# Masked keys and copies of halves on GpSimd instead of VectorE, in the head of a four-layer program on one core

## The chip, the cores and the metric

The program runs on one core of one Trainium2 chip. A core has five engines that run side by side, each with its own queue of instructions, which it takes in order: TensorE (PE; its weight loads are listed apart as PEld), VectorE (DVE), ScalarE (ACT), GpSimd (POOL) and SyncE (SP), which here only issues DMAs. Engines wait for each other by semaphores. The metric is the device time of one execution in microseconds (us), as the median of several runs.

## What is computed

The input x has 4 sequences of 2048 tokens with 256 features, all float32. Four layers follow one another, each on the layer-normalised x, and each is added to x:

```python
x = x + delta_attention(layernorm(x))   # conv, silu, l2norm, delta rule over time, 16 heads of 16
x = x + experts(layernorm(x))           # router: 8 of 32 experts a token, and a shared one
x = x + state_space(layernorm(x))       # a scan over time with 16 states
x = x + quantised_linear(layernorm(x))  # blocks of 32 rounded to a 6-bit grid
```

The change lies in the first. There every head keeps a 16 x 16 state S, and goes through the tokens:

```python
v_new = (v_t - k_t @ S) * beta_t
S = S + outer(k_t, v_new)
o_t = q_t @ S
```

## The kernel before

**Tiling.** The tokens are cut into 16 blocks of 128 tokens of each of the 4 sequences (512 rows). A block has 8 chunks of 16 tokens. Inside a chunk the delta rule is solved as a small triangular system, so that only the step from chunk to chunk is a recurrence: 128 steps in all.

**Stages of a block i in the first layer.**

- `project(i)`: loads x, normalises it, transposes it (TensorE), multiplies it by the three weights, and makes the short convolution of each on VectorE (`cy`, lines 259 and 263: one scaling and three multiply-adds of 128 x 512). The results are kq (keys and queries, interleaved) and vh (values).
- `gram(i)`: the products of all keys and queries of a chunk with its keys, head by head. Line 348 makes `kqd`, a copy of the keys and queries of a chunk, four times over, each time with all but one head's features masked to zero (kq, repeated, times hmask: 128 x 512). Sixteen such tiles are made for a block, in four groups of four (`u0`); there are three buffers for them. Eight small matmuls (line 358) read each one into `pg`. ScalarE brings `pg` to `gk`, of which there is one buffer, and a DMA stores `gk` in `gscr`. `gram(0)` runs inside `project(0)` ahead of the values' convolution, the others at the end of `project(i)`.
- `substitute(i)`: loads the products back as `lq`, sets the tile `e` to zero (a memset on GpSimd, line 396; one buffer, so the memset waits until the earlier `e` has been stored), and solves the triangular systems in 16 pairs of multiply and add on VectorE (`step`, line 416, and `e`, line 422). The result goes to `escr`.
- `chain()`: the recurrence. `prepare` (lines 469 to 523) loads the chunk's solved system (`tm`), makes `twice`, a copy of the chunk's values and keys in which every column stands twice (line 475, two copies of 128 x 256, one buffer), transposes it on TensorE (`vk`, line 484), masks it on ScalarE (`vkm`, `kr`), and multiplies by `tm` (`c0`, line 505). Then `wr`, `wt` and `wq` (lines 512 to 521) prepare the product with the state. `finish` adds that product (line 529), copies it out as `ro` (line 535, ScalarE), makes the update (`sps`, line 542), and writes the new `state` (line 549, VectorE). `prepare` of a step is written ahead of `finish` of the step before.
- `normalise` and `output`: after every four chunks, and at the end of the block (`x`, line 596).

**Other work in the same time.** `route(i)` chooses the experts of a finished block (written beside block i + 1 of the recurrence) and scatters its rows by 32 indirect DMAs that GpSimd issues (line 799). Experts' tiles come in from block 4 on; each ends in two indirect DMAs of GpSimd that add to the sums (line 967). After the last block of the recurrence come the remaining experts and the last two layers, where GpSimd also makes three elementwise operations a block (lines 1094, 1095 and 1147).

**What sets the order.** The stages are generators. `weave` draws steps from them in turn: beside block i of the chain, `substitute(i + 1)` and `project(i + 2)` (beside block 0 also `project(1)`). The block of instructions so written is then put in its final order on every engine by a scheduler that works with estimated durations, so a change of engine at one place can move instructions of all engines anywhere behind it. In the final program each engine's order is fixed. In addition `beside` makes the scatters of line 799 wait for a `mark`, the last `ro` written ahead of them, to spread them over the block.

**Names for the change.** `GROUPS = (3, 5, 5, 3)` groups the 16 blocks for the experts; `GFIRST` holds the first block of each group, so `GFIRST[1]` is 3.

Of the kernel before, what the change touches and what calls it, by code (L numbers as in the profile page):

```python
# [42 lines left out]
GFIRST = [sum(GROUPS[:g]) for g in range(NGRP)]  # L43
# [131 lines left out]
def delta_layer(ctx, sh, nblk, layer, done, others):  # L175
# [11 lines left out]
    nc, tc, a = sh.nc, sh.tc, sh.a  # L187
# [43 lines left out]
    def project(i):  # L231
# [84 lines left out]
        if i == 0:  # L316
            yield from gram(i)
# [9 lines left out]
        if i > 0:  # L327
            yield from gram(i)

    def gram(i):  # L330

        kq = keys[i]
        gscr = sh.dram.tile([NB * C, NF, NU, NP, 2, 2 * C], F32, name="gscr")
        for u0 in range(0, NK, 2):
            f, u = u0 // NU, u0 % NU
            gk = work.tile([P, 2, NP, 2, 2 * C], F32, name="gk", bufs=1)
            pairs = gk.rearrange("p u (c h q) r t -> p h u c (q r t)", c=NC2, h=2)  # L340
            pg = [
                layer.mm.tile([P, 2, NC2, HH * 2 * C], F32, name=f"pg{h}", tag="mm")
                for h in range(2)
            ]
            for du, c in itertools.product(range(2), range(NC2)):

                kqd = work.tile([P, NB, HH, 2 * C], F32, name="kqd", bufs=3)
                nc.vector.tensor_tensor(  # L348
                    kqd,
                    kq[:, u0 + du, c].rearrange("p b t w -> p b (t w)")  # L350
                    .unsqueeze(2).broadcast_to([P, NB, HH, 2 * C]),
                    hmask.unsqueeze(1).unsqueeze(3).broadcast_to([P, NB, HH, 2 * C]),
                    op=ALU.mult,
                )
                for h in range(2):
                    rows = slice(h * 64, (h + 1) * 64)
                    for b in range(NB):
                        nc.tensor.matmul(  # L358
                            pg[h][b * 32 : (b + 1) * 32, du, c],
                            kq[rows, u0 + du, c, b].rearrange("p t w -> p (t w)"),  # L360
                            kqd[rows, b].rearrange("p h t -> p (h t)"),
                            start=True, stop=True,
                        )
            for h in range(2):
                nc.scalar.copy(pairs[:, h], pg[h])
            nc.sync.dma_start(gscr[:, f, u : u + 2], gk[0:P:2])
            yield
        grams[i] = gscr
# [66 lines left out]
    def load_t(i, g):  # L435

        t = tm[g % 2]
        f, u = g // 2, g % 2 * 2
        for b in range(NB):
            l = (b * 32 + u * NP) * 2 * C  # L440
            nc.sync.dma_start(
                t[b * 32 : (b + 1) * 32, :, :, b % 2].rearrange("j u p t -> j (u p) t"),
                outer[i][f, :, l : l + 2 * NP * 2 * C].rearrange("j (l t) -> j l t", t=2 * C),
            )

    def chain():

        parts = {0: prepare(0, 0)}
        for i in range(nblk):
            ot = work.tile([P, NC2, NB, T], F32, name="ot", bufs=1)  # L450
            for k in range(NK):
                n = i * NK + k + 1
                if n < nblk * NK:
                    parts[n] = prepare(*divmod(n, NK))
                    yield
                if k % NU == 0:
                    ro = work.tile([P, NU, DM], F32, name="ro", bufs=2)
                with tc.high_priority():
                    finish(i, k, *parts.pop(n - 1), ro[:, k % NU, :])
                yield  # L460
                if k % NU == NU - 1:
                    normalise(k // NU, ro, qsq[i], ot)
                    yield
            output(i, ot)
            yield

    def prepare(i, k):
        if k % 2 == 0:
            load_t(i, k // 2)
        kq, vh = keys[i], vals[i]  # L470
        tmk = tm[k // 2 % 2][:, k % 2]

        twice = work.tile([P, 2, NC2, NB * C, 2], F32, name="twice", bufs=1)
        for w, src in ((0, vh[:, k]), (1, kq[:, k, :, :, :, 0])):
            nc.vector.tensor_copy(
                twice[:, w],
                src.rearrange("p c b t -> p c (b t)")
                .unsqueeze(3)
                .broadcast_to([P, NC2, NB * C, 2]),
            )  # L480
        vk = layer.turn.tile([P, 2, NC2, P], F32, name="vk", tag="tr")
        for w in range(2):
            for c in range(NC2):
                nc.tensor.transpose(
                    vk[:, w, c, :], twice[:, w, c].rearrange("p n r -> p (n r)"), sh.ident
                )
        vkm = work.tile([P, 2, NP, 2, HD], F32, name="vkm")
        pairs = vk.rearrange("p w c (q r d) -> p (w c q) r d", r=2, d=HD)
        for r in range(2):
            nc.scalar.activation(  # L490
                vkm.rearrange("p w q r d -> p (w q) r d")[:, :, r, :], pairs[:, :, r, :],
                AF.Copy, scale=parity[:, r : r + 1],
            )
        kr = work.tile([P, 2, DM], F32, name="kr")
        for h in range(2):
            nc.scalar.activation(
                kr[:, h, :], vk[:, 1].rearrange("p c d -> p (c d)"),
                AF.Copy, scale=kmask[:, h : h + 1],
            )

        c0 = pc.tile([P, 2, DM], F32, name="c0")
        for p in range(NP):
            for h in range(2):
                rows = slice(h * 64, (h + 1) * 64)
                nc.tensor.matmul(  # L505
                    c0[rows, :, p * 32 : (p + 1) * 32],
                    tmk[rows, p].rearrange("p b t -> p (b t)"),
                    vkm[rows, :, p].rearrange("p w r d -> p w (r d)"),
                    start=(p == 0), stop=False, skip_group_check=True,
                )  # L510
        wr = work.tile([P, DM], F32, name="wr", bufs=1)
        nc.scalar.copy(wr, c0[:, 1])
        wt = layer.turn.tile([P, NC2, NB, C, 2], F32, name="wt", tag="tr")
        for c in range(NC2):
            nc.tensor.transpose(
                wt[:, c].rearrange("p b t w -> p (b t w)"), wr[:, c * P : (c + 1) * P],
                sh.ident,
            )
        wq = work.tile([P, NC2, NB, C, 2], F32, name="wq")
        nc.scalar.mul(wq[..., 0], wt[..., 0], -1.0)  # L520
        nc.vector.tensor_tensor(
            wq[..., 1], kq[:, k, :, :, :, 1], wt[..., 1], op=ALU.subtract
        )
        return c0, wq, kr
# [817 lines left out]
```

## Time and profile before

| | |
|---|---|
| median of 9 runs | 3637.48 us (3624.57 to 3655.48) |
| the profiled execution's own time | 3648.82 us |
| its span | 3647.0 us |
| granted TensorE clock in it, mean | 0.873 |
| VectorE: kqd (line 348) | 256 instructions, 168.7 us, mean 689 ns |
| VectorE: twice (line 475) | 256 instructions, medians 288 and 295 ns |
| GpSimd: all | 1235 instructions, 1721.5 us |
| GpSimd: indirect DMAs (lines 799 and 967) | 512 at 1030 ns, 640 at 1635 ns |
| GpSimd: elementwise with two inputs of 128 x 1024 (lines 1094, 1095, 1147) | 48, means 2710, 2743, 2454 ns |

The profile is of one execution. It gives each instruction's start and duration on its engine, what released it when it waited, and the line of the program that it comes from. The page sums this up: busy time by engine, busy tenths in 40 equal slices of the span (each 91 us), groups of instructions. Any stretch, line or tile can be asked for by itself. An instruction's recorded duration holds the time in which it stands still on its engine after it has begun. Starts are in us from the span's start.

### The profile page before, as it was taken

The numbers are of one execution on the slowest core, as the hardware profiler recorded it, in microseconds if no ns is written. First come the engines' busy times: TensorE is split into PE (matmuls) and PEld (weight loads), VectorE is DVE, ScalarE is ACT, GpSimd is POOL, SyncE is SP. The second block draws the span as 40 slices with busy tenths as digits, with TensorE's granted clock in tenths as the row PEclk, the third lists the DMA queues.
The fourth block names the chain that finished last, engine by engine and source line by source line (L and its number), as shares of the span: only waits on it lengthen the run. The fifth ranks groups of instructions, "written<-read, shape, count | busy, mean of one in ns | idle before, by whom it ended". The sixth has DMA issues, their size and how long they took to land. (4 is left out here: it accounts for less than half of the span.)

```text
span 3647.0 us, 72319 instructions
## 1 busy us (share of the span) xinstructions
PE 2943.3 (81%) x24564; PEld 2184.2 (60%) x24564; DVE 2017.2 (55%) x4958; ACT 1812.3 (50%) x3640; POOL 1721.5 (47%) x1235
## 2 busy tenths in 40 slices
PE   5778887888988888888888878677488999789844
PEld 2455555665666666566666656566267677567612
DVE  4785775564646455464655535234367644475476
ACT  4454444454545444464545545334265766467522
POOL 0004322545454452545445454545566788658711
PEclk7777887998989888999989889888699999999967
DMA  3334446777878787787777788758699999999910
GB/s 88 54 61 129 113 113 171 189 182 187 193 196 206 179 209 179 192 199 196 194 185 190 174 224 203 197 159 239 188 315 285 269 303 294 312 272 281 234 64 18
DMA packets 788811, 695.92 MB, mean 191 GB/s; under 512 B 482313, under 2 KB 672025, under 8 KB 785305
## 3 DMA queue, kind: packets, MB, share of 16 engines
q1 hardware_dynamic: 669432, 522.25, 50.6%
q0 software_dynamic: 116736, 167.85, 22.5%
q8 instruction: 195, 3.19, 0.4%
q14 instruction: 176, 1.43, 0.1%
q10 hardware_dynamic: 2272, 1.19, 0.1%
HBM read 472.41 MB, written 267.53 MB: 203 GB/s over the span
## 5 line engine op out<-in xcount | busy, mean ns | idle before, releaser
L967 POOL DMA_INDIRECT sum<-ye,wrow x640 | 1046.6, 1635 | 956.5 <-ACT ye L964 746.5
L946 PE MATMUL gu<-xe,we 128*128 128x128 f32 x5120 | 710.0, 294 | 49.8 <-ACT xe L936 22.7
L799 POOL DMA_INDIRECT rows<-xn,rows x512 | 527.3, 1030 | 464.6 <-issue 242.9
L946 PEld LDWEIGHTS gu<-xe,we 128*128 128x128 f32 x5120 | 664.1, 207 | 113.3 <-issue 56.2
L959 PE MATMUL py<-we,he 128*128 128x256 f32 x1280 | 367.5, 412 | 85.0 <-DVE he L952 72.4
L952 DVE TENSOR_TENSOR he<-he,gu 128x256 f32<-128x256 f32 x320 | 133.3, 417 | 495.6 <-ACT he L951 370.4
L964 ACT ACTIVATE ye<-py,wrow 128x256 f32<-128x256 f32 x640 | 267.9, 471 | 279.0 <-PE py L959 146.2
L959 PEld LDWEIGHTS py<-we,he 128*128 128x128 f32 x1280 | 233.1, 200 | 147.8 <-DVE he L952 84.0
L951 ACT ACTIVATE he<-gu 128x256 f32<-128x256 f32 x320 | 123.1, 385 | 354.6 <-PE gu L946 203.7
L934 PE MATMUL px<-ident,xg 128*128 128x128 f32 x1280 | 227.4, 289 | 76.2 <-DMA xg<-rows 63.3
L505 PE MATMUL c<-vkm,tm 64*64 64x64 f32 x4096 | 213.2, 240 | 81.0 <-issue 70.2
L348 DVE TENSOR_TENSOR kqd<-kq,hmask 128x512 f32<-128x512 f32 x256 | 168.7, 689 | 188.8 <-PE pg L358 85.8
L936 ACT COPY xe<-px 128x512 f32<-128x512 f32 x320 | 188.1, 588 | 145.8 <-PE px L934 117.6
L934 PEld LDWEIGHTS px<-ident,xg 128*128 128x128 f32 x1280 | 165.7, 148 | 150.5 <-issue 60.6
L505 PEld LDWEIGHTS c<-vkm,tm 64*64 64x64 f32 x4096 | 170.9, 149 | 129.5 <-issue 108.0
L358 PE MATMUL pg<-kqd,kq 64*32 64x128 f32 x4096 | 184.3, 323 | 64.2 <-issue 46.0
L263 DVE SCALAR_TENSOR_TENSOR cy<-pre,convw,cy 128x512 f32<-128x512 f32 x288 | 215.0, 751 | 3.5
L549 DVE TENSOR_TENSOR state<-sps,same 128x512 f32<-128x512 f32 x254 | 165.9, 684 | 83.9 <-remote 36.3
L247 PE MATMUL proj<-xt,wqkv 128*128 128x512 f32 x384 | 206.0, 663 | 1.0 <-issue 0.8
L542 PE MATMUL sps<-ro,kr 64*128 64x128 f32 x2032 | 166.7, 310 | 18.3 <-ACT ro L535 18.3
L358 PEld LDWEIGHTS pg<-kqd,kq 64*32 64x32 f32 x4096 | 94.9, 119 | 137.1 <-issue 94.1
L542 PEld LDWEIGHTS sps<-ro,kr 64*128 64x128 f32 x2032 | 140.5, 210 | 51.9 <-ACT ro L535 25.0
(206 smaller groups left out, 4990.8 us busy)
## 6 DMA issues: line engine op xcount, KB each, us to landing
we<-in_wexp SPq DMA_DIRECT2D x640, 384.0 KB
xg<-rows SPq DMA_DIRECT2D x640, 128.0 KB
sum<-in_blank SPq DMA_DIRECT2D x48, 512.0 KB
part<-sum SPq DMA_DIRECT2D x48, 512.0 KB
rows<-in_zeros SPq DMA_DIRECT2D x132, 160.0 KB
x<-in_x SPq DMA_DIRECT2D x32, 512.0 KB
gscr<-gk SPq DMA_DIRECT2D x64, 256.0 KB
lq<-gscr SPq DMA_DIRECT2D x64, 256.0 KB
```

Of the source, the lines that this page charges most:

```text
L247: nc.tensor.matmul(ps, wqkv[:, k, w, c * P : (c + 1) * P], xt[:, k, :], start=(k == 0), stop=(k == NC2 - 1),)
L263: nc.vector.scalar_tensor_tensor(y, pre[:, :, k : k + T], convw[:, w, c, k : k + 1], y, op0=ALU.mult, op1=ALU.add,)
L358: nc.tensor.matmul(pg[h][b * 32 : (b + 1) * 32, du, c], kq[rows, u0 + du, c, b].rearrange("p t w -> p (t w)"), kqd[rows, b].rearrange("p h ...
L505: nc.tensor.matmul(c0[rows, :, p * 32 : (p + 1) * 32], tmk[rows, p].rearrange("p b t -> p (b t)"), vkm[rows, :, p].rearrange("p w r d -> p ...
L542: nc.tensor.matmul(sps[h][:, h2, c, :], kr[rows, h2, c * P : (c + 1) * P], ro[rows, c * P : (c + 1) * P], start=(i == 0 and k == 0 and h2 ...
L799: layer.beside(nc.gpsimd.indirect_dma_start(views[((i - GFIRST[GROUP_OF[i]]) * NB + b) * TOPK + k], bass.IndirectOffsetOnAxis(ap=rows[:, b ...
L934: nc.tensor.transpose(px[:, c, n, :], xg[:, n, c * P : (c + 1) * P], ident)
L936: nc.scalar.copy(xt, px)
L946: nc.tensor.matmul(gu[:, v, n, :], w[n][:, o : o + P], xt[:, c, n, :], start=(c == 0), stop=(c == NC2 - 1),)
L959: nc.tensor.matmul(py[:, n, :], h[:, n, :], w[n][:, 4 * P :], start=True, stop=True)
L964: nc.scalar.activation(y[:, n, :], py[:, n, :], AF.Copy, scale=wrow[:, n, 0:1])
L967: nc.gpsimd.indirect_dma_start(rt["sum"][g][(2 * t + n) % NACC][:, :], bass.IndirectOffsetOnAxis(ap=wrow[:, n, 1:2].bitcast(U32), axis=0), ...
```

## The change

Two instructions get another engine in some blocks: the masked keys and queries `kqd` of the grams 0 to 4 (80 instructions of 256), and the copies `twice` of the chain's blocks 0 to 3 (64 of 256). Operands, tiles and buffers stay.

```diff
             for du, c in itertools.product(range(2), range(NC2)):
 
                 kqd = work.tile([P, NB, HH, 2 * C], F32, name="kqd", bufs=3)
-                nc.vector.tensor_tensor(
+                (nc.gpsimd if i <= GFIRST[1] + 1 else nc.vector).tensor_tensor(
                     kqd,
                     kq[:, u0 + du, c].rearrange("p b t w -> p b (t w)")
                     .unsqueeze(2).broadcast_to([P, NB, HH, 2 * C]),
...
         twice = work.tile([P, 2, NC2, NB * C, 2], F32, name="twice", bufs=1)
         for w, src in ((0, vh[:, k]), (1, kq[:, k, :, :, :, 0])):
-            nc.vector.tensor_copy(
+            (nc.gpsimd if i <= GFIRST[1] else nc.vector).tensor_copy(
                 twice[:, w],
                 src.rearrange("p c b t -> p c (b t)")
                 .unsqueeze(3)
```

In the program that results, GpSimd's queue has a setup row ahead of the first `kqd` (the same kind stands ahead of the first of line 1094 before), and the order of all engines' instructions differs from the program before from the first gram on.

## The prediction

> **What bounds the kernel now.** I read the head of the page first, for how full each engine is and when. The first row is the busy time of each engine, the next ones the busy tenths in 40 slices of 91 us.
>
> ```profile
> span 3647.0 us, 72319 instructions
> ...
> PE 2943.3 (81%) x24564; PEld 2184.2 (60%) x24564; DVE 2017.2 (55%) x4958; ACT 1812.3 (50%) x3640; POOL 1721.5 (47%) x1235
> ...
> PE   5778887888988888888888878677488999789844
> ...
> DVE  4785775564646455464655535234367644475476
> ...
> POOL 0004322545454452545445454545566788658711
> ```
>
> The head is slices 1 to 7: VectorE (DVE) is nowhere fuller than in slice 3, GpSimd (POOL) is empty in the first three. The chain of waits is no help: its long pieces start at 2611 us. So I cut the head at the stores of each block (the additions of line 596 stand at 240.7, 358.2, 478.6 and 611.9 us) and asked for busy time by block. Columns: stretch, length, then busy us of PE, PEld, DVE, ACT, POOL.
>
> ```profile
> 84.00:242.00 158.00, 113.26 (x1311) 77.82 (x1312) 121.25 (x243) 82.78 (x171) 3.66 (x2) 0.77 0.35 62
> 242.00:361.00 119.00, 101.05 (x990) 69.35 (x988) 79.53 (x209) 53.75 (x119) 37.11 (x33) 0.78 0.42 108
> 361.00:480.00 119.00, 99.25 (x996) 67.67 (x994) 81.49 (x218) 53.59 (x119) 37.33 (x33) 0.80 0.41 107
> 480.00:612.00 132.00, 103.85 (x991) 69.55 (x990) 81.86 (x231) 53.42 (x117) 34.62 (x33) 0.77 0.55 146
> ```
>
> Block 0 is bound by VectorE as much as by anything (121 of 158 us; between 171 and 220 us its timeline has no gap). Blocks 1 to 3 are TensorE's, 79 to 85% busy. In block 0 TensorE waits 15.9 us for wq of VectorE; in blocks 1, 2 and 3 only 2.0, 3.2 and 3.5 us. Nothing fills time lost here: the experts start in block 4.
>
> The third view decides: what VectorE does while GpSimd computes. Before, that happens at a memset in the head and at three additions and products of the tail. Each pair below is one engine's row and the other's (start, duration).
>
> ```profile
> 214.31 1.83 POOL L396 MEMSET e<- 128x2080 f32 x1 [84.39 <-DMA escr<-e]
> ...
> 214.37 1.92 DVE L475 COPY twice<-vh 128x256 f32<-128x256 f32 x1
> ...
> 2640.01 2.95 POOL L1095 TENSOR_TENSOR x<-x,xn 128x1024 f32<-128x1024 f32 x1
> ...
> 2639.32 4.20 DVE L1040 TENSOR_TENSOR qd<-qr,qy 128x512 f32<-128x512 f32 x1
> ...
> 2752.10 2.90 POOL L1094 TENSOR_TENSOR xn<-xn,dvec 128x1024 f32<-128x1024 f32 x1
> ...
> 2752.00 3.29 DVE L1031 TENSOR_SCALAR qe<-qy 128x512 int32<-128x512 int32 x1
> ```
>
> The copy takes 0.29 us elsewhere, qd 0.69, qe 0.42. Each stood until GpSimd was done: **the two engines exclude each other** when VectorE copies, scales, or combines two operands from SBUF. Reductions (line 1019, 0.68 us) and products with one operand in PSUM (line 952, 0.42 us) keep their time beside the same GpSimd rows.
>
> **The change, part by part.** 80 masks (kqd; grams 0 to 4) and 64 copies (twice; blocks 0 to 3) leave VectorE. Their price there:
>
> ```profile
> L348 DVE TENSOR_TENSOR kqd<-kq,hmask 128x512 f32<-128x512 f32 x32 | 20.9, 686 | 1.0 <-ACT kq L293 0.7 <-PE pg L358 0.2
> ```
>
> (block 0), and 0.29 us a copy.
>
> *Price on GpSimd.* No such row exists. The nearest is the product 128x1024: 2.36 us alone, 2.89 median with collisions. Half of it, as a kqd has half the elements, is 1.18 to 1.45 us; I take 1.45, since VectorE is busy. For a copy of 256 elements: from the memsets (12 elements 0.11 us, 2080 elements 1.95 us) 0.33 us, from the product's rate 0.72; I take 0.45, nearer to the memset, which has one stream as a copy has one input.
>
> *Price on VectorE of a collision.* Five collisions with the product (4.20, 3.29, 3.86, 3.73, 3.57 us against 0.69, 0.42, 0.69, 0.69, 0.42) lose 0.24 us more than GpSimd's own recorded time, on average. So a kqd on GpSimd that meets a colliding instruction costs VectorE 1.45 + 0.24 = 1.7 us, a copy 0.7; one that meets none costs 0.
>
> *How often.* In block 0 the colliding kinds that stay (cy 26.7 and 5.8, step 18.3, e 18.2, lq 3.7, vh 2.8 us) hold 75.5 of 158 us, 48%. Over 1.45 us about two instructions of VectorE begin, so I take 1 - 0.52 x 0.52 = 0.73. In blocks 1 to 3 they hold 112 of 370 us, 30%: 1 - 0.7 x 0.7 = 0.51. Bounds 0 and 1.
>
> *Block 0.* Freed: 20.9 + 20 x 0.29 = 26.7 us. Lost: 0.73 x (32 x 1.7 + 20 x 0.7) = 50 us. Net 23 us more for the fullest engine. With 23% idle some is absorbed; I take 0.6 of it, **+14 us** (bounds -15 and +40, the latter at collision always).
>
> *Blocks 1 to 3.* Blocks 1 and 2 free 16 x 0.66 + 16 x 0.3 = 15.4 us each and lose 0.51 x (16 x 1.7 + 16 x 0.7) = 19.6; block 3 (copies alone) frees 4.8, loses 5.7. Net +9 us on an engine with a third idle: half, **+5 us** (bounds -6, +15).
>
> *Gram 0*, with nothing beside it, is on the path (the first lq load is issued at 78.0 us behind it). VectorE is ahead: four kqd take 2.5 us, groups start at 59.45, 62.27, 65.79, 69.92, paced by the single gk buffer and its store. On GpSimd four take 4.8 to 5.8 us, more than the pace; three are made ahead by buffers. 13 from 58.3 us end at 73.9 to 77.2, where the last ended at 70.6 and its matmul at 73.7. **+3 us** (0 to +7). The setup row that the new program puts ahead of the first kqd costs nothing by the trace: ahead of line 1094 it takes 0.04 us and the product follows at once. It would be covered anyway, from 34 us to the second kqd at 52 us. The Trainium skill (GPSIMD Engine Reference, Instruction dispatch) gives a freshly loaded kernel's first call some 6 us; the row above does not show it, and by the rule the sum would still be the same because of that cover.
>
> *GpSimd's queue.* It is in order, and three things that wait stand in it: the memset of e (until escr has been stored), ten scatters that wait for rows, and runs of six or eight scatters (1.28 us apart) that wait for ro, the mark. Behind them now stand kqd and twice, and behind those TensorE, in its own fixed order. Comparing the orders of the two programs: in block 1 a kqd that VectorE made at 318.6 us, beside eight scatters (317.95 to 328.7), now follows them; gram 3 ends a step or two later; several transposes vk stand behind the matmuls with the state instead of ahead. The copy has cover, it runs two steps ahead of ro (343.6 us for a step whose accumulator comes free at 360.4), and a gram has a block's. I take 2 to 3 us a block for short stops, **+7 us** in three (0 to +25, at the latter a run of eight scatters, 10 us, uncovered nearly once a block). Scatters that VectorE stops in turn wait off the path: GpSimd has 37 of 119 us busy, about 70 after.
>
> Sum: 14 + 5 + 3 + 7 = **+29 us**. The profiled execution took 3648.82 us (span 3647.0); it would be 3678. The median of the runs is 11 us lower, 3637.48, so 3666. What the head loses, the rest starts later by; I expect no repayment.
>
> The Trainium skill (SBUF - State Buffer, Who interferes with whom) has the same exclusion but says that whoever starts first keeps the port. The rows above speak against it: qd had begun 0.69 us before GpSimd's row and still ended 0.56 us after it. By the page half the collisions would cost GpSimd instead, block 0 would lose 25 us against 27 freed, blocks 1 to 3 some 22 against 36, and the sum would be near +3.
>
> **Rivals.**
> 1. *VectorE is relieved after all.* The mechanism is the price of a collision in block 0: below 0.39 (26.7 / 68.4) collisions per GpSimd instruction VectorE gains. For it: GpSimd has 3.66 us of work there, and 14 kqd and 8 copies stand in the stretch without gaps. Then 14 x 0.65 + 8 x 0.29 = 11 us go there, and 2 to 3 us of waits for wq in each of three blocks: -18, **3620**. Against it: the stretch holds step, e and cy, all colliding.
> 2. *It cancels*: collisions at the page's rate and a well covered queue, from -11 to +11: **3640**.
> 3. *TensorE stands behind GpSimd's queue*: kqd uncovered behind scatters and memsets, and collisions always: 40 + 15 + 7 and half of the queue's bound, 13, make +75, **3712**; it decides from about +50 on.
>
> That the move does not happen is no rival: the program's order shows the instructions on GpSimd.
>
> **How the numbers follow.** Forecast (+11 to +50) 0.50, rival 1 0.15, rival 2 0.21, rival 3 0.14. Bounds of the terms: -21 to +87. The range 3622 to 3712 leaves out about half of rival 1 and half of rival 3. About 0.3% (11 us) is what a measurement of this kernel can tell from no change: faster 0.15, same 0.21, slower 0.64.
>
> **What will show it.** Right: kqd on POOL at 1.2 to 1.9 us; beside it cy, step and e at 1.5 to 2.5 us instead of 0.7; DVE's busy time in block 0 not lower despite 52 fewer instructions; block 0 ending 10 to 25 us later, blocks 1 to 3 longer by 2 to 8 us each; later blocks as long as now. Wrong: cy and step keep 0.75 and 0.55 us (then rival 1), or waits of pg for POOL far above 10 us a block (rival 3). A reordering of the later program that moves the tail by itself would make the prediction wrong without touching its reasons.

## The result and the profile after

The changed kernel takes 3670.15 us (median of 20 runs, 3645 to 3694), the kernel before in the same runs 3641.98 us (62 runs): 1.0078 times as long, 95% interval [1.0061, 1.0094], or 28 us more. The profiled execution of the changed kernel took 3658.95 us with a span of 3657.2 us; that of before lies 10 us below it.

The head of its page, as shown for before: busy time of each engine, then tenths in 40 slices, here of 91 us.

```profile
span 3657.2 us, 72416 instructions
...
PE 2940.7 (80%) x24564; PEld 2172.1 (59%) x24564; DVE 1976.8 (54%) x4814; ACT 1824.8 (50%) x3647; POOL 1850.9 (51%) x1379
...
PE   5777876889888888998888887777489999789944
...
DVE  3674555555646464664646555233367544475476
...
POOL 2225333345454544546454444545576788658711
```

VectorE has lost 144 instructions and 40 us, GpSimd has gained 144 and 129 us; GpSimd's first three slices are no longer empty. VectorE's slices 2 and 3, which were 7 and 8, are 6 and 7, and its slices 5 and 6 have gone from 7 to 5. Cut at the stores of the blocks, as before (stretch, length, then busy us of PE, PEld, DVE, ACT, POOL, the granted clock, the share and the GB/s of the DMAs):

```profile
84.00:242.30 158.30, 112.62 (x1276) 74.44 (x1276) 104.02 (x183) 85.07 (x172) 49.39 (x55) 0.75 0.33 61
242.30:373.70 131.40, 101.40 (x1067) 70.92 (x1066) 73.89 (x189) 58.40 (x128) 62.02 (x67) 0.81 0.38 99
373.70:506.80 133.10, 104.08 (x997) 70.25 (x996) 72.38 (x185) 54.34 (x120) 59.17 (x65) 0.76 0.38 96
506.80:644.30 137.50, 99.66 (x923) 66.54 (x923) 80.37 (x220) 50.39 (x109) 37.21 (x41) 0.74 0.54 142
```

Block 0 is hardly longer than before (its store comes at 242.3 us instead of 240.7), though VectorE has 17 us less to do in it (121.25 to 104.02). Counted from store to store, blocks 1 and 2, which were 117.4 and 120.4 us, are 131.4 and 133.1, and block 3 is 137.5 instead of 133.3. The added time of this pair is in blocks 1 to 3: 30.8 us. That is not where the prediction's largest term lay.

What the moved instructions cost on GpSimd in block 0 (line, operation, shapes, count; busy us, mean ns):

```profile
L348 POOL TENSOR_TENSOR kqd<-kq,hmask 128x512 f32<-128x512 f32 x32 | 36.8, 1166 | 56.3 <-ACT pre L255 29.9 <-PE pg L358 12.8 <-DVE state L549 7.2
L475 POOL COPY twice<-vh 128x256 f32<-128x256 f32 x11 | 5.1, 461 | 44.9 <-PE vk L484 32.5 <-DVE vh L322 12.4
L475 POOL COPY twice<-kq 128x256 f32<-128x256 f32 x10 | 4.9, 493 | 0.0
```

A mask alone takes 1.04 us (the median of 79 in the head; 0.69 on VectorE), a copy alone 0.40 (0.29). The rest of the means is collisions. The longest row of them, VectorE's side first, then GpSimd's (start, duration):

```profile
204.64 0.80 DVE L422 TENSOR_TENSOR e<-e,step 128x432 f32<-128x432 f32 x1
205.36 1.52 DVE L263 SCALAR_TENSOR_TENSOR cy<-pre,convw,cy 128x512 f32<-128x512 f32 x1
206.80 1.37 DVE L416 TENSOR_TENSOR step<-lq,e 128x364 f32<-128x364 f32 x1
208.09 1.52 DVE L263 SCALAR_TENSOR_TENSOR cy<-pre,convw,cy 128x512 f32<-128x512 f32 x1
```

```profile
204.94 4.13 POOL L348 TENSOR_TENSOR kqd<-kq,hmask 128x512 f32<-128x512 f32 x3
```

Three masks in 4.13 us instead of 3.1, three instructions of VectorE at 1.37 to 1.52 us instead of 0.55 to 0.75: **they take turns**, and each pays for a part. One collision costs VectorE about 0.7 us in the mean (its time over the median of the same instruction), and 12 to 14 of block 0's 32 masks meet one, depending on where the line is drawn.

### The profile page after: what moved, and what is told of

Same layout as the page of the kernel before. It is cut to its first block, busy times and chain, and to the rows that moved or that the text cites. A ratio compares the mean times of both kernels' runs of the same rounds, so it can differ in the third digit from the quotient of the medians.

```text
span 3657.2 us, 72416 instructions
## 1 busy us (share of the span) xinstructions
PE 2940.7 (80%) x24564; PEld 2172.1 (59%) x24564; DVE 1976.8 (54%) x4814; ACT 1824.8 (50%) x3647; POOL 1850.9 (51%) x1379
## 5 line engine op out<-in xcount | busy, mean ns | idle before, releaser
L946 PE MATMUL gu<-xe,we 128*128 128x128 f32 x5120 | 697.6, 290 | 42.6 <-issue 24.3
L946 PEld LDWEIGHTS gu<-xe,we 128*128 128x128 f32 x5120 | 649.5, 203 | 105.7 <-issue 63.3
L348 DVE TENSOR_TENSOR kqd<-kq,hmask 128x512 f32<-128x512 f32 x176 | 116.7, 689 | 154.3 <-PE pg L358 75.3
L542 PEld LDWEIGHTS sps<-ro,kr 64*128 64x128 f32 x2032 | 139.4, 209 | 66.1 <-ACT ro L535 43.6
L358 PEld LDWEIGHTS pg<-kqd,kq 64*32 64x32 f32 x4096 | 91.7, 118 | 134.1 <-issue 85.0
```

The costliest lines, as they stand in the source:

```text
L358: nc.tensor.matmul(pg[h][b * 32 : (b + 1) * 32, du, c], kq[rows, u0 + du, c, b].rearrange("p t w -> p (t w)"), kqd[rows, b].rearrange("p h ...
L542: nc.tensor.matmul(sps[h][:, h2, c, :], kr[rows, h2, c * P : (c + 1) * P], ro[rows, c * P : (c + 1) * P], start=(i == 0 and k == 0 and h2 ...
L946: nc.tensor.matmul(gu[:, v, n, :], w[n][:, o : o + P], xt[:, c, n, :], start=(c == 0), stop=(c == NC2 - 1),)
```

## The experiments

The same kernel took very different times in the three sessions of these runs: the kernel before had medians of 3618.34 us (first four kernels), 3360.42 us (the next four) and 3365.01 us (the last four), at granted clocks of about 0.87, 0.90 and 0.90. So every kernel is given as a ratio to the kernel before beside it, and profiles are compared within the last two sessions.

### Which part: masks or copies, early or late

Masks alone, the copies left on VectorE (`kqd_only`), and copies alone (`twice_only`); these edits and those of the next pair are shown against the changed kernel:

```diff
-            (nc.gpsimd if i <= GFIRST[1] else nc.vector).tensor_copy(
+            nc.vector.tensor_copy(
```

```diff
-                (nc.gpsimd if i <= GFIRST[1] + 1 else nc.vector).tensor_tensor(
+                nc.vector.tensor_tensor(
```

> Only the masks (kqd of grams 0 to 4) go to GpSimd, the copies stay on VectorE. Three theories for the +28 us of the whole change. Collisions (VectorE stands while GpSimd reads): the masks have nearly all of that time, so this run should lose 20 to 28 us. Queue (TensorE stands behind masks and copies that stand behind scatters on GpSimd): the loss splits, 10 to 20 us here. Order (the scheduler lays the instructions of blocks 1 and 2 differently, and the recurrence's waits are covered worse): the parts need not add up; this run can lie anywhere from -10 to +30, and its block times will not follow the number of GpSimd instructions in the block.

> Only the copies (twice of blocks 0 to 3) go to GpSimd, the masks stay on VectorE. Collisions: 0 to +5 us, since a copy takes 0.4 us there. Queue: +10 to +20 us, since a copy stands ahead of the transposes of the recurrence and here behind sixteen scatters. Order: anything from -10 to +20; the TensorE order is nearer to that of before than that of the whole change.

The change in the grams 0 to 2 and the copies of block 0 alone (`early`), and the rest of it alone, the grams 3 and 4 and the copies of the blocks 1 to 3 (`late`):

```diff
-                (nc.gpsimd if i <= GFIRST[1] + 1 else nc.vector).tensor_tensor(
+                (nc.gpsimd if i <= 2 else nc.vector).tensor_tensor(
...
-            (nc.gpsimd if i <= GFIRST[1] else nc.vector).tensor_copy(
+            (nc.gpsimd if i <= 0 else nc.vector).tensor_copy(
```

```diff
-                (nc.gpsimd if i <= GFIRST[1] + 1 else nc.vector).tensor_tensor(
+                (nc.gpsimd if 3 <= i <= 4 else nc.vector).tensor_tensor(
...
-            (nc.gpsimd if i <= GFIRST[1] else nc.vector).tensor_copy(
+            (nc.gpsimd if 1 <= i <= 3 else nc.vector).tensor_copy(
```

> The change only where GpSimd has no scatters: masks of grams 0 to 2, copies of block 0. The prologue should end 4 to 5 us later in the trace, as with the whole change, and block 0 give 3 us of it back. Collisions: two thirds of the masks are here, so +15 us or more. Queue: nothing stands behind a scatter, so 0 to +5 us. Order: from block 1 on the order is much like that of before, so 0 to +5 us.

> The change only where GpSimd has scatters: masks of grams 3 and 4, copies of blocks 1 to 3. Collisions: about +8 us. Queue: nearly the whole loss, +20 to +28 us, in blocks 1 and 2. Order: TensorE's order differs from before about as much as that of the whole change does; a loss of like size is likely (+10 to +30), though in other blocks perhaps.

| kernel | median, us | ratio | interval |
|---|---|---|---|
| masks alone | 3664.72 | 1.0127 | [1.0081, 1.0173] |
| copies alone | 3618.48 | 1.0002 | [0.9976, 1.0028] |
| early part | 3625.61 | 1.0014 | [0.9990, 1.0037] |
| late part | 3639.70 | 1.0062 | [1.0032, 1.0091] |

The copies cost nothing that could be told. The masks do, and not where VectorE is full: the early part, which has the 48 masks of the prologue and block 0 and their collisions, is within what can be told from no change. That speaks against collisions, which were expected to cost 15 us or more there. The late part alone is slower by 21 us, as the queue's theory expected (20 to 28), and early and late together (1.4 and 6.2 thousandths) nearly make the whole (7.8). But the queue's theory missed twice: the copies alone should have cost 10 to 20 us by it, and masks alone, at +46 us, come out above the whole change and above every expectation. The interval is wide, and why they should be worse than masks and copies together stays open. So does the path of the late part's loss: in its profile TensorE waits for no mask in blocks 1 and 2.

### Is it the new order, or the engines?

The scheduler gave TensorE another order, so the change is two changes. The next four kernels part them. In `held` the masks and copies are on GpSimd, but TensorE's instructions stand exactly in the order of before; in `reversed` all is on VectorE, and TensorE's stand in the order of the changed kernel. Both add, after the program of the other kind has been built for its order, dependences that bind each TensorE instruction to the one ahead of it and need no semaphore:

```diff
...
+        names = [n for n in names if n in traced]
+        for a, b in zip(names, names[1:]):
+            tc.add_manual_dep(
+                traced[b], a,
+                mybir.DependencyInfo(
+                    mybir.DependencyClass.NoSync, mybir.DependencyReason.DATA
+                ),
...
```

> The whole change, masks and copies on GpSimd, but TensorE's instructions are held in exactly the order that they have in the program before (edges that fix the order of issue alone). Order theory (the loss comes from the new interleaving on TensorE): the loss goes away, -10 to +8 us. Queue theory (TensorE stands behind masks and copies that stand in GpSimd's queue): the loss stays or grows, +28 us or more, and TensorE's waits for POOL become its largest in blocks 1 and 2. Collision theory: +28 us, as GpSimd runs the same instructions beside the same work of VectorE.

> The other way round: masks and copies on VectorE as before, but TensorE held in exactly the order that it has in the changed program. Order theory: the loss is here without any GpSimd work, +20 to +40 us, with blocks 1 and 2 each 10 us longer or more. Queue and collision theories: about 0, -8 to +8 us.

`shadow` is the kernel before, in which GpSimd makes the 80 masks once more into a tile that nothing reads: collisions without a relief for VectorE, and without a wait of TensorE for GpSimd.

```diff
+                if i <= GFIRST[1] + 1:
+                    idle = work.tile([P, NB, HH, 2 * C], F32, name="idle", bufs=1)
+                    nc.gpsimd.tensor_tensor(
+                        idle,
...
```

> Everything as before on VectorE; in addition GpSimd makes the masks of grams 0 to 4 once more, into a tile that nothing reads. TensorE's order is that of before. It adds GpSimd's work, the collisions with VectorE and the delay of the scatters behind it, relieves nobody, and lets nobody wait for GpSimd's result. Collision theory: +28 us or more, since VectorE is not relieved either. Order theory: 0 to +8 us. Queue theory: 0 to +8 us.

The changed kernel itself ran again beside these (`after_again`), unedited.

> The changed kernel unaltered, on the same chip as the three others, so that they are compared with it there: +20 to +36 us by every theory. If it comes out well above, near the +46 us of the masks alone, then that run's excess over the whole change was the chip's.

| kernel | work on | TensorE's order | median, us | ratio | interval |
|---|---|---|---|---|---|
| before | VectorE | before | 3360.42 | 1 | |
| `held` | GpSimd | before | 3390.51 | 1.0091 | [1.0067, 1.0115] |
| `reversed` | VectorE | after | 3360.65 | 1.0000 | [0.9981, 1.0020] |
| `after_again` | GpSimd | after | 3385.49 | 1.0075 | [1.0049, 1.0101] |
| `shadow` | both | before | 3386.52 | 1.0069 | [1.0043, 1.0095] |

The order is worth nothing that could be told (7 us either way) and the engines are worth 25 to 30 us, in either order. The theory that the scheduler's order is the cause has fallen for these kernels. `shadow` shows that collisions do cost when nothing is freed: its block 0 ends at 265.9 us (`reversed`: 230.6), with 147 us of VectorE's work in it. Its 26 us are as many as those of the change, and the queue's theory had expected 0 to 8. What tells the two apart is where they lie: blocks 1 to 3 take 356.4 us in `shadow`, 348.2 in `reversed` and 366.0 in `after_again`. In the changed kernel the relief of VectorE stands against its collisions.

`reversed` and `after_again` have the same 24,564 matmuls in the same order, so their traces can be laid side by side. `reversed` first, then `after_again`, each cut at the blocks' stores:

```profile
84.00:230.60 146.60, 105.50 (x1270) 72.37 (x1269) 115.73 (x232) 81.73 (x169) 3.67 (x2) 0.79 0.34 63
230.60:345.90 115.30, 96.08 (x1068) 67.81 (x1067) 84.66 (x222) 58.87 (x128) 34.90 (x33) 0.85 0.43 109
345.90:453.70 107.80, 90.38 (x998) 62.06 (x997) 84.52 (x217) 53.86 (x120) 36.28 (x33) 0.86 0.46 118
453.70:578.80 125.10, 88.95 (x924) 60.15 (x923) 82.18 (x228) 50.22 (x109) 39.70 (x33) 0.80 0.61 155
```

```profile
84.00:242.30 158.30, 113.23 (x1277) 74.48 (x1276) 103.44 (x182) 85.28 (x173) 49.34 (x55) 0.75 0.34 62
242.30:361.30 119.00, 95.59 (x1068) 67.55 (x1067) 73.85 (x189) 58.42 (x128) 60.64 (x67) 0.84 0.43 109
361.30:475.60 114.30, 94.46 (x998) 63.91 (x997) 71.52 (x186) 54.41 (x120) 57.73 (x65) 0.84 0.43 112
475.60:608.30 132.70, 89.92 (x923) 61.61 (x922) 80.37 (x219) 50.18 (x109) 42.38 (x41) 0.78 0.58 147
```

Blocks 0 to 3 are 11.7, 3.7, 6.5 and 7.6 us longer, 29.5 together; at the end of the spans 28.1 are left (3356.3 and 3384.4 us). Of the 29.5, TensorE is idle for 17.2 (the gaps ahead of its instructions in these blocks sum to 113.9 and 131.1 us) and busy for 12.3 more (380.9 and 393.2 us) with the same instructions but six, at a lower granted clock. The idle time by what ended it:

| TensorE's wait, blocks 0 to 3 | reversed, us | after_again, us | difference |
|---|---|---|---|
| pg for a mask of GpSimd | 0 | 16.9 | +16.9 |
| vk for a copy of GpSimd | 0 | 1.4 | +1.4 |
| product with the state for wq of VectorE | 34.8 | 23.6 | -11.2 |
| route's transpose for xn of VectorE | 2.6 | 10.3 | +7.7 |
| sps for ro of ScalarE | 12.8 | 16.6 | +3.8 |
| all others | 63.7 | 62.3 | -1.4 |

So VectorE's relief does reach TensorE: the chain's product waits 11.2 us less for it, though not in block 0 (12.2 and 13.2 us) but in blocks 1 to 3 (22.6 and 10.4). The waits for masks take more than that back: 5.0 us in block 0, 6.5 and 5.4 in blocks 1 and 2. What GpSimd was doing ahead of the two longest, in `after_again`, with the matmul that followed behind each (start, duration, operation, and in brackets the idle time before it and what ended it; a count behind a mask is of masks in a row):

```profile
228.63 1.83 POOL L396 MEMSET e<- 128x2080 f32 x1 [3.20 <-DMA escr<-e]
230.42 2.04 POOL L348 TENSOR_TENSOR kqd<-kq,hmask 128x512 f32<-128x512 f32 x2
```

```profile
231.51 0.68 PE L358 MATMUL pg<-kqd,kq 64*32 64x128 f32 x16 [4.70 <-POOL kqd L348]
```

```profile
341.51 0.97 POOL L799 DMA_INDIRECT rows<-xn,rows  x1 [0.30 <-PE pg L358]
342.79 1.33 POOL L799 DMA_INDIRECT rows<-xn,rows  x1 [0.30 <-issue]
344.42 0.97 POOL L799 DMA_INDIRECT rows<-xn,rows  x1 [0.30 <-issue]
345.42 1.05 POOL L348 TENSOR_TENSOR kqd<-kq,hmask 128x512 f32<-128x512 f32 x1
```

```profile
346.52 0.68 PE L358 MATMUL pg<-kqd,kq 64*32 64x128 f32 x16 [4.55 <-POOL kqd L348]
```

At 229 us the mask stands behind the memset, which waited for the store of the earlier `e`; at 345 us behind a run of scatters. TensorE starts within 0.06 us of the end of the first mask both times. Neither wait was ended by VectorE.

### GpSimd's queue without the scatters

If masks are late because scatters stand ahead of them, the loss must go with the scatters. Both kernels were run without the 96 scatters of the routes 0 to 2 (those beside the blocks 1 to 3), the same parts left out in each (`quiet_before`, `quiet_after`):

```diff
-                layer.beside(nc.gpsimd.indirect_dma_start(
...
+                if i >= GFIRST[1]:
+                    layer.beside(nc.gpsimd.indirect_dma_start(
...
+            if i == GFIRST[1] - 1:
+                nc.vector.memset(state["count"], 0.0)
```

> The kernel before without the scatters of line 799 in routes 0 to 2 (96 of 512 indirect DMAs; they stand on GpSimd beside blocks 1 to 3), and with the counts of the first group set to zero, so that all its tiles read the spare rows. The rows of the first three blocks are so left out of the experts' sums; work of the experts keeps its size. It is the partner of the next kernel. Each theory expects that it takes about as long as the kernel before, within 20 us: on VectorE's side nothing waits for these scatters.

> The changed kernel without the same 96 scatters, with the same parts left out as in its partner, the kernel before without them. Queue (a mask stands behind runs of scatters, and TensorE behind the mask): blocks 1 to 3 together lose at most 5 us against the partner, instead of the 18 to 30 us of the pairs with scatters, and no matmul of a gram waits more than 2 us for a mask in blocks 1 and 2; the whole is +8 to +15 us, from the first 240 us. Collision (VectorE stands for GpSimd): masks and copies collide as often without scatters, blocks 1 to 3 lose 15 us or more, the whole +25 to +30 us.

`quiet_before` took 3351.05 us (0.9960, [0.9943, 0.9977] of the kernel before), `quiet_after` 3345.55 us (0.9944, [0.9925, 0.9963]). Against each other the change now gives -5 us, with 9 either way (the means of six runs each): of the loss of 25 us nothing is left that could be told. `quiet_before`, then `quiet_after`:

```profile
84.00:243.00 159.00, 112.05 (x1278) 77.23 (x1277) 121.01 (x242) 83.62 (x171) 3.66 (x2) 0.76 0.37 64
243.00:347.80 104.80, 88.90 (x993) 62.62 (x991) 78.42 (x209) 52.94 (x119) 1.83 (x1) 0.85 0.31 69
347.80:455.30 107.50, 91.74 (x1013) 64.08 (x1012) 80.99 (x218) 54.12 (x120) 1.83 (x1) 0.84 0.35 73
455.30:582.60 127.30, 93.24 (x1019) 64.25 (x1017) 83.20 (x235) 53.84 (x117) 1.83 (x1) 0.81 0.51 123
```

```profile
84.00:241.00 157.00, 107.34 (x1274) 71.63 (x1274) 102.65 (x180) 84.81 (x172) 49.72 (x55) 0.77 0.32 58
241.00:347.30 106.30, 90.11 (x998) 63.60 (x998) 71.86 (x186) 56.18 (x121) 27.78 (x33) 0.87 0.36 77
347.30:447.40 100.10, 84.91 (x997) 59.57 (x996) 71.92 (x186) 55.87 (x121) 27.57 (x33) 0.91 0.34 73
447.40:574.80 127.40, 94.74 (x1050) 66.16 (x1048) 84.83 (x232) 54.96 (x119) 8.46 (x11) 0.83 0.56 128
```

GpSimd still makes the masks (27.8 us of masks, copies and one memset in block 1), VectorE still meets them (its instructions lose about 17 us in the head, as much as in the changed kernel), and the blocks are at most 1.5 us longer than without the change, or shorter. The same question to the trace, what ended the idle time ahead of the grams' matmuls from 242 to 500 us, in `held`, in `after_again` and in `quiet_after`:

```profile
its engine sat idle before it (us, times) until:
  POOL kqd L351: 32.0, 9
```

```profile
its engine sat idle before it (us, times) until:
  POOL kqd L348: 11.9, 6
```

```profile
its engine sat idle before it (us, times) until:
  POOL kqd L348: 0.5, 2
```

This also fits `held`, which is no better than the changed kernel: in the old order TensorE comes to the masks before they are there, and waits 20 us more for them. At the end of block 3 `held` is 16.6 us behind `after_again` (624.9 and 608.3 us), at the end of the spans 5.4. The expectation that 8 to 15 us from the first 240 us would stay was wrong: in the scheduler's own order block 0 is not longer with the change (157.0 against 159.0 us). With other TensorE orders in the two quiet kernels this pair is not as strict as the one before; but the order by itself was worth nothing there. And it takes away all that masks and scatters do to each other on GpSimd: that the masks' lateness is the whole of it is not shown by it. Nor can it speak for the 11.7 us of block 0 in the strict pair, since no scatter stands beside block 0.

### Gram 0, and more buffers

`gram0_back` is the changed kernel with gram 0's masks on VectorE, `buffers` the changed kernel with seven buffers for `kqd`:

```diff
-                (nc.gpsimd if i <= GFIRST[1] + 1 else nc.vector).tensor_tensor(
+                (nc.gpsimd if 1 <= i <= GFIRST[1] + 1 else nc.vector).tensor_tensor(
```

```diff
-                kqd = work.tile([P, NB, HH, 2 * C], F32, name="kqd", bufs=3)
+                kqd = work.tile([P, NB, HH, 2 * C], F32, name="kqd", bufs=7)
```

> The changed kernel with the sixteen masks of gram 0 on VectorE again. Prologue (gram 0 has nothing beside it, so slower masks lengthen the way to the first state): the last mask of gram 0 comes 3 to 4 us earlier, the first copy of the state's product 5 to 7 us, and the whole is 5 to 7 us below the changed kernel, +20 to +23 us on the kernel before. Collision: as long as the changed kernel, about +28 us, since no other work of VectorE stands beside gram 0.

> The changed kernel with seven buffers for kqd instead of three. If the loss is the mask's own length and delay behind three buffers, GpSimd can now make four more ahead, the waits of TensorE for masks go, and the whole is +8 to +15 us on the kernel before. Queue: the masks keep their places behind the scatters in GpSimd's fixed order, which the scheduler sets again, so a part of it goes at most: +15 to +28 us. Collision: no fewer instructions meet, +25 to +30 us.

`gram0_back`: 3385.47 us, 1.0061 [1.0047, 1.0076], too near to 1.0075 to be told apart by the times. The profile tells more: gram 0's last mask ends 3.8 us earlier than in `after_again` (71.4, 75.2 us), the first `ro` starts 2.6 us earlier (141.4, 144.0), and block 0 ends 0.6 us earlier (241.7, 242.3). The lead is lost at the wait for the mask behind the memset at 231 us, which is still there (4.8 us). So in these profiles gram 0's delay does not outlast block 0; the 5 to 7 us that were expected of the first `ro` and of the whole did not come.

`buffers`: 3391.34 us, 1.0074 [1.0053, 1.0095], nothing gained. Blocks 1 to 3 together are 349.6 us (`after_again` 366.0, `reversed` 348.2), and TensorE waits 3.4 us for masks in them instead of 11.9: masks made further ahead do seem to shorten them. But in the program that the scheduler then made, which has another order, block 0 ends at 254.2 us instead of 242.3, with 5.5 us of waiting for a copy at 91.7 us that `after_again` does not have. The expected gain came and was lost again.

## Why the prediction was right, and where it was not

Forecast +29 us and 3666, measured +28 and 3670.15. The sum was right and its makeup was not: the terms of collisions were too large, that of the queue too small, and that the two errors cancelled is luck. In the original profiles the prologue and block 0 lost 1.6 us where 17 had been put, blocks 1 to 3 lost 30.8 where 12 had been put, and 22 of these 32 us were no longer there at the end. Of the times set as signs (VectorE no less busy in block 0, that block 10 to 25 us later, blocks 1 to 3 longer by 2 to 8 us each) only block 3's came, 4.2 us.

- **Block 0, +14 by collisions: this step failed.** It put 50 us of loss on VectorE against 26.7 freed. Measured, VectorE loses about 9 us to collisions in block 0 of the changed kernel (the time of its instructions over their own medians), and is 17 us less busy. Both factors were too high: 1.7 us for a mask, measured about 0.7; a rate of 0.73, measured 12 to 14 of 32. The price came from five collisions with a product of 2.4 us, in which VectorE stood for all of it; with 1.04 us masks in a row the two take turns. In blocks 1 and 2 the rate was 4 to 6 of 16 (0.51 taken), so the +5 there was too high too. VectorE so lost less than it was freed of, which is what rival 1 needed, and its mechanism worked in part: VectorE was relieved, and in the pair with one order waits for wq fell by 11.2 us, though in blocks 1 to 3 and not in block 0. Its result did not follow. Block 0 does get 11.7 us longer in that pair: TensorE is idle 4.0 us more, with 5.0 us of waits for masks, 4.7 of it for the one behind the memset, and busy 7.7 us more at a lower clock (0.79, 0.75). Between the two original programs it is 1.6 us.
- **GpSimd's queue, +7: the size too small, the mechanism right as far as it is shown.** Without the scatters nothing of the loss is left, so it hangs on them. Blocks 1 to 3 lost 17.8 us in the pair with one order and 30.8 between the original profiles; the bound was 25. The direct waits for masks are 11.9 us of the 17.8, and in the original profiles 0.5 of the 30.8. The step held that a gram has cover for a block's length and called short stops 2 to 3 us a block. What the cover lacked, by the waits and by `buffers`: a gram's sixteen masks have three buffers, so GpSimd can't use it ahead of time, and a run of scatters in between is a stop. Rival 3, with the same mechanism, set "waits of pg for POOL far above 10 us a block" as its sign; measured were 5 to 6.5 us a block.
- **Gram 0, +3:** the last mask came at 73.8 us, as worked out (73.9 to 77.2 for its end, measured 74.8). But in the profile of `gram0_back` the delay is hidden later, so it seems to have no place in the sum; the times can't tell.
- **Prices on GpSimd:** 1.04 us alone and 1.17 with collisions (1.45 taken, bounds 1.18 to 1.45), 0.40 for a copy (0.45 taken). The mask is faster than half of the larger product.
- **No repayment:** right in the pair with one order (29.5 us at block 3, 28.1 at the end). The two original profiles are 32.4 us apart there and 10.2 at the end; single executions of either kernel spread by more than that, and what made this one good is not shown.
- **The rule that spoke against it.** The Trainium skill (SBUF - State Buffer, Who interferes with whom) let the first comer keep the port, and by it the estimate was near +3. The five rows of before that were held against it don't settle who came first: beside each an indirect DMA of GpSimd, begun earlier, was still running (2638.97 to 2640.57 us beside qd at 2639.32). For masks in a row the trace agrees with it better than with the step that was taken: both engines' rows are lengthened (1.38 us for 1.04, 1.37 to 1.52 us for 0.55 to 0.75). What it could not tell is the loss itself, which goes with the scatters in GpSimd's queue.

Not shown: that the later start of `xn` (+7.7 us, VectorE's) comes from GpSimd, and whether the lower clock follows TensorE's stalls or is a cause by itself. Nor is it shown what made the 30.8 us of the original pair. In the original changed profile all 768 matmuls of the grams in blocks 1 to 3 are recorded, and this is what ended TensorE's idle time ahead of them (us and times):

```profile
L358 PE MATMUL pg<-kqd,kq x768: 266/293/419, 323.5 to 634.9; 64*32 64x128 f32 x192
...
its engine sat idle before it (us, times) until:
  ACT gk L365: 7.5, 3
  DVE kqd L348: 1.2, 1
  POOL kqd L348: 0.5, 1
```

But for 0.5 us the masks were there in time. TensorE is as busy in these three blocks as before (305.1 us both times) and idle for 96.8 us instead of 66.1; what grew most are the waits of `sps` for `ro` in block 1 (2.0 to 9.8 us) and waits ahead of `c` in block 2 that nothing in the profile explains (0 to 10.9). So the reading that masks come late rests on the last two sessions, and for the original runs it is carried over.

## What to carry to other kernels

Before moving work to an idle engine, read its queue and not its load: GpSimd was 31% busy in blocks 1 and 2, but its instructions were scatters that wait for a mark, and in the last two sessions what was put behind them made TensorE wait, although VectorE, from which the work came, was truly relieved. The early part, with no scatters beside it, cost nothing that could be told; the late part, among the scatters, cost 21 us. A change that also lets a scheduler reorder is parted by a 2 x 2: each kind of work in each order.

## What the runs showed of the hardware

- VectorE and GpSimd take turns when both run instructions of about 1 us one behind the other: 1.37 to 1.52 us on VectorE for work of 0.55 to 0.75, 1.38 in the mean on GpSimd for 1.04.
- The same matmuls (4,260, but for six at the cuts) kept TensorE busy 12.3 us longer over four blocks in which it idled 17 us more and the granted clock was 0.01 to 0.04 lower.
- One kernel, the one before, had medians of 3642, 3618, 3360 and 3365 us in four sessions. In the longer ones, waits of TensorE that nothing in the profile explains stand in blocks 1 to 3 (ahead of pg and c 22.6 us in the profile of before, none in `reversed`), and ScalarE waits up to 10.6 us for signals whose sender is not recorded.
